# Buffers by name, a mask in the first norm, paired squares and a new order in a two-layer convolution block

## The chip, the cores and the metric

The kernel runs on one core of a Trainium2 chip. The metric is the device time of one execution in microseconds (us), a median over several runs; the profile is of one further execution. The engines are TensorE (PE; PEld is its weight load), VectorE (DVE), ScalarE (ACT), GpSimd (POOL) and SyncE (SP), which here issues the DMAs. All data are float32; a float32 product appears in the trace as two records of PE.

## What is computed

The input x has the shape 4 x 128 x 128 x 128 (batch, channel, row, column). Layer 0 is, cut to what matters:

```python
def _block(t):                       # t: tokens (pixels) x 128 channels
    t = _ln(t)                       # with gain ln0_g and shift ln0_b
    y1 = _ln(t)
    t = t + (sigmoid(y1) * y1) @ W_out.T
    wht = _ln(t) @ W_whiten.T
    k = square(relu(wht @ W_key.T))  # 512 wide
    return t + sigmoid(wht @ W_recep.T) * (k @ W_value.T)

x = x + _L0(_gn(x))                  # _gn: group norm, 32 groups of 4 channels
x = x + _L1(_gn(x))                  # 3x3 convolution times a gate of the means
```

`_L0` adds the block of the image and the block of the turned image, turned back; since the block works on each pixel alone, both are the same. Layer 1 is a 3x3 convolution with a bias, multiplied by a squeeze-and-excite gate.

## The kernel before

An image of the batch has 16384 pixels: 32 chunks of 512 pixels. Two chunks make a group g (64 groups, 16 for each image). `layer0(g)` emits the operations of a group, once for each of its two chunks h: the group norm's scale and shift on a copy of the block that is loaded with its pixels turned (`u`, tile xd), a 32x32 transpose on DVE (`ut`), three layer norms (`bn0` to `bn2` on DVE, then eps on ACT, a power -0.5 on POOL, the shift on POOL), each norm applied by ACT (`t`, `z`), gain and bias (`g`, `b`), a transpose of z on PE (`Tz`) or, from group 22 on, through DRAM, silu on ACT, the attention product (`att`), and then on [channel, pixel] tiles: four key products (`pk`, 128 x 512), relu on ACT (`re`), squares on ACT or DVE (`sq`, `sqd`), the receptance product (`pr`) with its tanh on ACT (`th`, tile r), four value products (`kv`) that accumulate into one bank, the gate on DVE (`q`), and two additions into the resident block of x on POOL (`S`, `x1`). `R` is the reciprocal deviation of the third norm spread over all partitions. For groups 0 and 1 the gain and bias stand on DVE instead of POOL.

Before group 0 the statistics of image 0 are needed. `first_stats` loads it as eight tiles xf of 1 MB and DVE takes their statistics (`in0`); after tiles 6 and 7 it also emits three and two "hot" products on PE, which read the tile, write into a bank called fill and serve no result. `input_norm(b)` turns the statistics of an image into a scale and a shift: `gag` aggregates per channel (DVE), `gpm` averages the means over groups of 4 channels (PE), `gsp` forms mean squares (DVE), `gpv` averages these (PE), then eps, power and shift. Since the turned block needs the values of four channel quarters in four columns, `gpm` and `gpv` multiply by four matrices `gturn[:, q]`, one product for each column; `gpm` has a fifth product by `gmat`. The images 1 to 3 get their norm while the image before is worked on.

`conv_setup(b)` does the like for layer 1 and scales its weights, and `conv(k)` computes the convolution of a block of 16 rows by a transform over rows: DVE forms v0 to v5, PE multiplies (three products of about 512 columns each, tile m), ACT and DVE put the outputs together, SP stores. Convolution blocks of image b run among the groups of image b + 1; those of the last image run alone at the end, where tiles v are put into slots of the pool h and products into the banks of all the pools (TAIL_BANKS).

The order of all this is not written by hand. Each operation is registered with an engine, a cost, a priority (its group number plus an entry of the table SHIFT for its kind), what it reads and writes, and the tiles that it opens. `Plan.order` plays the program with these costs, always takes for the engine that comes free next the operation with the best priority among those that can start soon (LOOK and HASTE weigh lateness), and the instructions are emitted in this order, each engine's in its own queue. The semaphores follow from the data. ROOM gives the number of buffers of each pool. In the order of before, the buffers of a pool are taken in turn: the k-th tile of a pool waits until the tile that was opened ROOM[pool] places earlier is free. While the planned time is below 330 us, `busy` puts fill products (of `gturn` by `gmat`) into the planned gaps of PE, except ahead of `gpm` and the hot products.

SQUARES says for each chunk h and key product j whether the square is done on DVE ("D") or ACT ("A"): in groups 0 to 16 j = 0, 1 on DVE and j = 2, 3 on ACT, later all on ACT, each as an operation of its own on 512 elements in a tile h of which there are six.

Lines that the prediction names: L411 fill, L493 aggregate, L498 and L500 the products of the first norm, L509 to L527 its small steps, L757 the scale on ACT, L820 powers, L839 the layer norms applied, L942 the transpose of z, L954 att, L1033 pk, L1038 relu, L1044 and L1050 the square on ACT and on DVE, L1058 pr, L1063 tanh, L1071 kv, L1080 the gate, L1086 and L1026 additions on POOL, L1182 a v of the convolution, L1203 to L1205 its products. The core of `input_norm` before:

```python
def grouped(key, src, own):
    pm = T[key]
    for q in range(SUB):
        nc.tensor.matmul(pm[:, q : q + 1], gturn[:, q], src, start=True, stop=True)
    if own:
        nc.tensor.matmul(pm[:, SUB : SUB + 1], gmat, src, start=True, stop=True)
```

Of the kernel before, what the change touches and what calls it, by code (L numbers as in the profile page):

```python
# [13 lines left out]
P = 128  # L14
# [9 lines left out]
    "R": -94.694, "Rc": 15.085, "Rm": -2.646, "S": 24.009, "T": -84.8, "Tz": -36.19, "W": -22.14,  # L24
    "ab": 37.315, "att": 1.644, "b": 31.731, "bn0": 11.794, "bn1": -17.35, "bn2": -15.592,
    "bx": 49.609, "c": 7.82, "cag": 6.719, "cav": -18.068, "cd": -103.804, "cp": -37.768,
    "cp1": -27.368, "cpm": -17.233, "cpr": -71.755, "cpv": -65.194, "cre": 48.407, "crt": -73.005,
    "csg": -26.086, "csp": -39.311, "cth": -29.247, "cve": 53.942, "e": 12.136, "e0": 14.7,
    "e1": -70.81, "e2": -55.971, "edge": 60.492, "fw": 14.887, "g": -16.106, "gag": -13.379,
    "gnb": -14.148, "gpm": -2.701, "gpv": -23.531, "grt": -1.635, "gsp": -6.989, "gve": -30.013,  # L30
    "hot": -13.329, "in": 26.361, "in0": 105.375, "kv": 3.816, "late": 12.753, "m0": 23.5,
    "m1": -101.213, "o": -54.585, "pk": 3.497, "pq": -18.954, "pr": 3.288, "q": -106.007,
    "raw": -61.508, "rc": -6.337, "re": -93.796, "silu": -97.676, "sq": -115.033, "sqd": -34.912,
    "t": -2.49, "tD": -49.255, "tR": 16.588, "tW": -20.948, "th": -60.823, "tt": 105.266,
    "u": 16.271, "us": -19.465, "ut": 67.807, "ut2": 9.337, "uw": -50.513, "v": 57.985, "w": 117.982,
    "w0": 44.736, "w1": -43.048, "w2": -6.943, "x": 70.181, "x1": -70.076, "xc": 6.78, "xd": 2.407,
    "xf": -58.371, "xo": -10.863, "xs": -54.606, "y": 24.867, "z": 15.121, "zD": 21.243,
    "zR": 18.813, "zW": -13.966,
}
SQUARES = (("DDAA", "DDAA"), ("AAAA", "AAAA"))  # L40
# [3 lines left out]
LOOK = {'PE': 0.018, 'DVE': 0.087, 'ACT': 0.048, 'POOL': 0.004, 'SP': 0.048}  # L44
HASTE = 31.975
SQUARES_AT = 17
ROOM = dict(
    x=3, xd=2, xs=2, ut=3, t=7, z=2, y=2, zd=2, zc=2, td=2, tt=2, R=2, y2=2, h=6, r=2, xc=2, vt=3, v=4,
# [3 lines left out]
BACKLOG = 1.96  # L52
FIRST_U_ON_DVE = (2, 3)


XF_BUS, FIRST_XD, LATE_AT = 3.4, -25, -5
FILL_UNTIL, FILL_STEP = 330, 1.2
FIRST_FILL = {6: 3, 7: 2}
# [30 lines left out]
class Plan:  # L89
# [34 lines left out]
    def order(self):  # L124
# [14 lines left out]
        freed, queue, taken = {}, {}, {}  # L139
# [12 lines left out]
        def slots(o):  # L152
            at = 0.0
            count = {}
            for t in o["new"]:
                tag = self.home[t]
                k = taken.get(tag, 0) + count.get(tag, 0)
                count[tag] = count.get(tag, 0) + 1
                if k >= self.room[tag]:
                    old = queue[tag][k - self.room[tag]] if k - self.room[tag] < len(queue[tag]) else None  # L160
                    if old is None or pending[old]:
                        return INF
                    at = max(at, freed[old])
            return at

        while done < n:
# [54 lines left out]
            for t in o["new"]:  # L221
                tag = self.home[t]
                queue.setdefault(tag, []).append(t)
                taken[tag] = taken.get(tag, 0) + 1
            for t in touches[i]:
                pending[t] -= 1
                freed[t] = max(freed.get(t, 0.0), en)
            for j in after[i]:
                reach = (self.OWN if ops[j]["eng"] == e else self.REACH)[ops[j]["eng"]]
                ready[j] = max(ready[j], en + reach)  # L230
                left[j] -= 1
                if not left[j]:
                    waiting[ops[j]["eng"]].append(j)
# [9 lines left out]
def conv_preact_kernel(  # L243
# [42 lines left out]
        z=[P, SUB, C], y=[P, CH], y2=[P, CH], h=[P, CH], r=[P, CH],  # L286
# [10 lines left out]
    def make(t, tag):  # L297
        pool = ps if tag[0] == "B" else sb
        T[t] = pool.tile(SHAPE[tag], F32, tag=tag, name=t[0], bufs=ROOM[tag])
        return T[t]  # L300

    def bank(name):
        return ps.tile([P, CH], F32, tag="Bh", name=name, bufs=ROOM["Bh"])

    def staged(name, n, src=None):
        t = sb.tile([P, n], F32, tag="h", name=name, bufs=ROOM["h"])
        if src is not None:
            nc.scalar.dma_start(t, src)
        return t

    vec = sb.tile([5, C], F32, tag="vt", name="vec", bufs=ROOM["vt"])
# [3 lines left out]
    for name, src in (("g0row", ln0_g), ("b0row", ln0_b)):  # L315
        row0.append(sb.tile([1, C], F32, tag="y2", name=name, bufs=ROOM["y2"]))
# [3 lines left out]
    wo = sb.tile([P, P], F32, tag="v", name="wo", bufs=ROOM["v"])  # L320
# [26 lines left out]
    gmat = gmat.rearrange("p a b -> p (a b)")  # L347
    gturn = const.tile([P, SUB, P], F32, tag="gturn", name="gturn")
    for q in range(SUB):
# [3 lines left out]
        )  # L353

# [10 lines left out]
    ones = sb.tile([1, P], F32, tag="r", name="ones", bufs=ROOM["r"])  # L365
    nc.gpsimd.memset(ones, 1.0)

    warm = sb.tile([P, 1], F32, tag="r", name="warm", bufs=ROOM["r"])
# [38 lines left out]
    fill = ps.tile([P, CH], F32, tag="Bconv", name="fill", bufs=ROOM["Bconv"])  # L407
# [14 lines left out]
    READ, WRITE = (0, 0.85), (0, 0.4)  # L422

    def op(name, eng, cost, prio, emit, reads=(), writes=(), new=(), port=False, bus=0.0):
        return plan.op(name, eng, cost, prio + SHIFT.get(name, 0.0), emit, reads, writes, new, port, bus)
# [58 lines left out]
    def input_norm(b, at):  # L484
# [5 lines left out]

        def aggregate():
            S["mv"] = col("mv0", 2)
            nc.vector.bn_aggr(S["mv"], st0.pop(b).rearrange("p n s -> p (n s)"))  # L493

        def grouped(key, src, own):
            pm = T[key]
            for q in range(SUB):
                nc.tensor.matmul(pm[:, q : q + 1], gturn[:, q], src, start=True, stop=True)  # L498
            if own:
                nc.tensor.matmul(pm[:, SUB : SUB + 1], gmat, src, start=True, stop=True)  # L500

        def means():
            make(("pm0", b), "Bh")
            grouped(("pm0", b), S["mv"][:, 0:1], True)

        def spread():
# [5 lines left out]
            S["q"] = q  # L512

        def variances():
            make(("pv0", b), "Bh")
            grouped(("pv0", b), S["q"], False)
# [12 lines left out]

        step("gag", V, (0.4, 0.5), aggregate, [(s, i) for i in range(NCH)], [(("gnv", b), 0)])  # L530
        step("gpm", E, (0.5, 0.55), means, (), [(("pm0", b), 0)], [(("pm0", b), "Bh")])
        step("gsp", V, (0.65, 0.75), spread, [(("pm0", b), 0)])
        step("gpv", E, (0.4, 0.45), variances, (), [(("pv0", b), 0)], [(("pv0", b), "Bh")])
# [4 lines left out]
    def conv_setup(b, at):  # L538
# [7 lines left out]
        def small(name, eng, cost, fn, bank=None):  # L546
            t = (name, b)
            step(name, eng, cost, fn, (), [(t, 0)] if bank else (), [(t, "Bh")] if bank else ())
# [58 lines left out]
        small("csp", V, (0.8, 0.9), spread)  # L607
        small("cpv", E, (0.1, 0.15), variances, True)
        small("cve", V, TINY, with_eps)
# [3 lines left out]
        small("cre", V, (0.2, 0.3), rect)  # L613
        small("cpr", E, (0.3, 0.35), second, True)
        small("cth", A, (0.6, 0.75), tanh)
# [120 lines left out]
    def layer0(g):  # L736
# [3 lines left out]
        if p * PAIR % PER == 0:  # L740
# [6 lines left out]
            for q in range(SUB):  # L747

                on_dve = k == 0 and q in FIRST_U_ON_DVE

                def lay(q=q, on_dve=on_dve):
                    rs, nb = gn0[b]
                    scale, bias = rs[:, q : q + 1], nb[:, q : q + 1]
                    if on_dve:
                        nc.vector.tensor_scalar(T[xd][:, q], T[xd][:, q], scale, bias, ALU.mult, ALU.add)
                    else:
                        nc.scalar.activation(T[xd][:, q], T[xd][:, q], AF.Identity, bias=bias, scale=scale)  # L757

                op(
                    "u", V if on_dve else A, (0.61, 0.7) if on_dve else (0.705, 0.82), g, lay, [(("gn0", b), 0), *((xd, a) for a in range(SUB))],  # L760
                    [(xd, ("u", q))],
                )
# [11 lines left out]
        def norm(n, src):  # L774
            st, rs, nb = ("st", n, g), ("rs", n, g), ("nb", n, g)
            eps = ceps[:, 0:1] if n == 0 else ceps[:, 1:2]
            for h in range(PAIR):
                op(
# [3 lines left out]
            if n == 2 and not R_ON_PE(g):  # L782
# [13 lines left out]
                def store(a):  # L796
                    if a == 0:
                        T[rd] = dram.tile([SUB, N, 32], F32, tag="rd", name="rd", bufs=ROOM["rd"])
# [12 lines left out]
            for hs in parts:  # L811
                part = slice(hs[0] * SUB, (hs[-1] + 1) * SUB)
# [30 lines left out]
        def to_channels(name, src, td, tc_, h):  # L843
# [16 lines left out]
            def store(a):  # L860
                if a == 0:
                    T[ds_] = dram.tile([P, SUB, PAIR, P], F32, tag=name + "s", name=name + "s", bufs=ROOM[name + "s"])
# [17 lines left out]
        for h in range(PAIR):  # L880
            r = (p * PAIR + h) % PER

            def turn(h=h, r=r):
# [5 lines left out]
                "ut", V, (0.61, 0.7), g, turn, [(xd, ("u", q)) for q in range(SUB)],  # L889
# [3 lines left out]
        for h in range(PAIR):  # L893
            t = ("t", g, h)
# [21 lines left out]
        for h in range(PAIR):  # L916
            t, z, zt, y, att = (("t", g, h), ("z", g, h), ("zt", g, h), ("y", g, h), ("att", g, h))
# [8 lines left out]
        for h in range(PAIR):  # L926
            t, z, zt, y, att = (("t", g, h), ("z", g, h), ("zt", g, h), ("y", g, h), ("att", g, h))
# [36 lines left out]
        if R_ON_PE(g):  # L964
            for h in range(PAIR):
                rp = ("rp", g, h)
# [22 lines left out]
        for h in range(PAIR):  # L989
            r = (p * PAIR + h) % PER  # L990
# [4 lines left out]
        for h in range(PAIR):  # L995
# [325 lines left out]
```

## Time and profile before

| | |
|---|---|
| median of 3 runs | 1744.41 us (1743.2 to 1745.63) |
| the profiled execution | 1742.63 us |
| its span, first to last instruction | 1740.9 us |
| granted TensorE clock, mean | 0.997 |
| PE records kv, pk (1024 each), busy | 525.8 and 480.9 us |
| PE records of the convolution (L1203 to L1205), busy | 588.0 us |
| PE records att, pr, busy | 132.8 and 132.3 us |
| ACT relu (512) and square (444), busy | 336.1 and 267.5 us |
| DVE square (68), mean | 740 ns |
| DMA | 354.66 MB, 204 GB/s |

Busy times are unions of records; a record of a product is longer than its step to the next[...]. Idle time of an engine that is not the bound costs nothing. The waits that the views name are put down to the semaphore that came last.

### The profile page before, as it was taken

Reading aid. Unit: us, or ns where it says so; the run is one execution under the profiler, and the core shown is the slowest. Engines: PE = TensorE matmul, PEld = TensorE weight load, DVE = VectorE, ACT = ScalarE, POOL = GpSimd, SP = SyncE. Lnnn points to the kernel's source line nnn. Section 1 sums busy time; section 2 is a strip of 40 time slices with the busy share of each in tenths; the row PEclk is TensorE's granted clock in tenths of the full one; section 3 lists DMA queues with packets and bytes.
Section 4 is the critical chain, followed back from the end, with each engine's and each line's share of the span. In section 5 each row is a group of like instructions: output and inputs, shape, how many; then the busy total and the mean of one; then the engine's idle time right before and its main releaser. Section 6 shows DMA issues by size and latency. Waiting matters only on the chain.

```text
span 1740.9 us, 18709 instructions
## 1 busy us (share of the span) xinstructions
PE 1690.7 (97%) x4872; PEld 815.7 (47%) x4872; DVE 1424.9 (82%) x2619; ACT 1293.8 (74%) x2656; POOL 1184.0 (68%) x1085
## 2 busy tenths in 40 slices
PE   5899999999999999999999999999999999999999
PEld 2444544444444445444445445454544444444443
DVE  5898888788889967798998887888897766448986
ACT  1999998898988887889889877998887875440000
POOL 1778887788987885879777886988878773310000
PEclk9999999999999999999999999999999999999999
DMA  9366675466577777578778877577776565215321
GB/s 326 91 213 202 193 219 194 145 206 230 153 250 246 252 230 236 199 232 247 250 245 245 254 238 240 178 218 236 241 254 199 183 204 176 101 75 224 154 98 73
DMA packets 140170, 354.66 MB, mean 204 GB/s; under 512 B 19079, under 2 KB 78750, under 8 KB 122782
## 3 DMA queue, kind: packets, MB, share of 16 engines
q1 hardware_dynamic: 139472, 352.99, 63.1%
q8 instruction: 39, 0.64, 0.2%
q14 instruction: 69, 0.57, 0.1%
q10 hardware_dynamic: 590, 0.46, 0.1%
HBM read 230.31 MB, written 123.07 MB: 203 GB/s over the span
## 4 chain that ended last, share of the span: by engine, by line
PE 71%; ACT 10%; POOL 8%; DVE 7%; DMA 2%; issue 2%; SPq 0%; ACTq 0%; DVEq 0%; POOLq 0%
PE kv L1071 19%; PE pk L1033 18%; PE m L1203 7%; PE m L1204 7%; PE m L1205 7%; PE att L954 5%; PE pr L1058 5%; ACT t L839 2%; ACT h L1038 2%; POOL rs L820 2%; ACT z L839 2%; DVE st L770 1%; ACT h L1044 1%; POOL x L1026 1%; POOL t L908 1%
## 5 line engine op out<-in xcount | busy, mean ns | idle before, releaser
L1071 PE MATMUL kv<-h,wv 128*128 128x512 f32 x1024 | 525.8, 598 | 4.6 <-DVE r L1080 2.6
L1033 PE MATMUL pk<-y,wk_s 128*128 128x512 f32 x1024 | 480.9, 595 | 4.7 <-ACT h L1038 3.1
L1038 ACT ACTIVATE h<-pk,kbias 128x512 f32<-128x512 f32 x512 | 336.1, 682 | 90.9 <-PE pk L1033 88.3
L1033 PEld LDWEIGHTS pk<-y,wk_s 128*128 128x128 f32 x1024 | 190.0, 190 | 239.3 <-issue 178.1
L1071 PEld LDWEIGHTS kv<-h,wv 128*128 128x128 f32 x1024 | 183.0, 190 | 205.3 <-issue 164.1
L1044 ACT ACTIVATE h<-h 128x512 f32<-128x512 f32 x444 | 267.5, 629 | 2.6
L1086 POOL TENSOR_TENSOR x<-x,r 128x512 f32<-128x512 f32 x128 | 169.8, 1327 | 132.0 <-DVE r L1080 128.5
L820 POOL TENSOR_TENSOR rs<-rs,nhalf 128x8 f32<-128x8 f32 (+1 forms) x134 | 227.2, 1700 | 47.3 <-ACT rs L817 45.1
L839 ACT ACTIVATE z<-t,nb,rs 128x128 f32<-128x128 f32 x512 | 208.7, 489 | 21.8 <-POOL nb L825 20.9
L839 ACT ACTIVATE t<-ut,nb,rs 128x128 f32<-128x128 f32 x512 | 209.7, 488 | 8.5 <-POOL nb L825 4.8
L908 POOL TENSOR_TENSOR t<-t,g 128x512 f32<-128x512 f32 x124 | 161.2, 1301 | 68.0 <-ACT t L839 67.6
L770 DVE BATCH_NORM_STATS2 st<-t 128x6 f32<-128x256 f32 x512 | 187.1, 410 | 22.9 <-POOL t L911 22.7
L1203 PE MATMUL m<-v,uw 128*128 128x512 f32 x384 | 197.7, 596 | 3.9 <-DVE v L1182 3.9
L1204 PE MATMUL m<-v,uw 128*128 128x508 f32 x384 | 195.4, 590 | 0.0
L1205 PE MATMUL m<-v,uw 128*128 128x508 f32 x384 | 194.9, 589 | 0.0
L1015 POOL TENSOR_TENSOR y<-tt,R 128x512 f32<-128x512 f32 x96 | 130.9, 1367 | 59.8 <-PE pk L1033 46.9
L1026 POOL TENSOR_TENSOR x<-tt,x 128x512 f32<-128x512 f32 x124 | 162.5, 1324 | 3.9 <-DMA tt<-ts 3.7
L911 POOL TENSOR_TENSOR t<-t,b 128x512 f32<-128x512 f32 x124 | 162.7, 1319 | 2.6
L954 PEld LDWEIGHTS att<-wo,y 128*128 128x128 f32 x1024 | 130.9, 192 | 51.7 <-issue 33.1
L1063 ACT ACTIVATE r<-pr,rbias 128x512 f32<-128x512 f32 x128 | 87.1, 681 | 72.6 <-PE pr L1058 36.2
L1058 PE MATMUL pr<-y,wr_s 128*128 128x512 f32 x256 | 132.3, 600 | 3.9 <-ACT h L1038 3.0
L954 PE MATMUL att<-wo,y 128*128 128x128 f32 x1024 | 132.8, 276 | 0.4 <-ACT y L947 0.3
(160 smaller groups left out, 2278.6 us busy)
## 6 DMA issues: line engine op xcount, KB each, us to landing
xd<-in_x SPq DMA_DIRECT2D x128, 256.0 KB
x<-in_x SPq DMA_DIRECT2D x32, 1024.0 KB
xo<-x SPq DMA_DIRECT2D x32, 1024.0 KB
R<-rd SPq DMA_DIRECT2D x63, 512.0 KB
ts<-td SPq DMA_DIRECT2D x248, 128.0 KB
tt<-ts SPq DMA_DIRECT2D x62, 512.0 KB
out<-xc SPq DMA_DIRECT2D x31, 1024.0 KB
xc<-xo SPq DMA_DIRECT2D x24, 1152.0 KB
```

Source lines behind the costliest of these rows:

```text
L770: nc.vector.bn_stats(st[:, i : i + 2, :].rearrange("p n f -> p (n f)"), two)
L820: nc.gpsimd.tensor_tensor(T[rs][:, part], T[rs][:, part], nhalf[:, :k], ALU.pow)
L839: nc.scalar.activation(dst[:, s, :], src[:, s, :], AF.Identity, bias=nb[:, i : i + 1], scale=rs[:, i : i + 1])
L954: nc.tensor.matmul(pa[:, ts(m, P)], T[y][:, ts(m, P)], wo2, start=True, stop=True)
L1033: nc.tensor.matmul(make(pk, "Bh"), wk_s[:, ts(j, P)], T[y2], start=True, stop=True)
L1038: nc.scalar.activation(make(hh, "h"), T[pk], AF.Relu, bias=kbias[:, j : j + 1])
L1044: nc.scalar.activation(T[hh], T[hh], AF.Square)
L1058: nc.tensor.matmul(make(pr, "Bh"), wr_s, T[y2], start=True, stop=True)
L1071: nc.tensor.matmul(T[kv], wv[:, j, :], T["h", g, h, j], start=(j == 0), stop=(j == NH - 1))
L1203: nc.tensor.matmul(pc, u[:, 1], vv, start=True, stop=False)
L1204: nc.tensor.matmul(pc[:, :, 1:W], u[:, 0], vv[:, :, 0 : W - 1], start=False, stop=False)
L1205: nc.tensor.matmul(pc[:, :, 0 : W - 1], u[:, 2], vv[:, :, 1:W], start=False, stop=True)
```

## The change

It consists of these parts.

- Each tile of a pool is bound to a slot that `Plan.order` chose: the plan keeps a list of free slots of each pool with the time at which each came free, takes the earliest one, and the tile is then allocated under the slot's own name with one buffer. The setup's tiles take slots in turn (`early`); the staged weights go into the pool t instead of h.
- The first norm multiplies the channel means by a mask `own` (128 x 4, one column for each quarter of 32 channels) and uses one product by `gany`, the sum of the four `gturn` matrices, where it had four products. The planner's costs of these steps change too.
- The hot products are gone (`FIRST_FILL` is empty).
- Tiles h hold two key products side by side (three tiles of 1024 in place of six of 512). SQUARES gets a form "W": one ACT instruction squares both halves. Groups 0 to 16: "DAWW" for chunk 0, "DDWW" for chunk 1; later groups "WWWW".
- LAG lowers the priority number of the chunks of groups 0 and 1, chunk by chunk, so that they go first.
- The tiles v of the last image's convolution lie in slots of t.
- The steps of `conv_setup` name their bank among what they read. The scale `u` is registered by row piece; with the values set it is emitted as before (two quarters on ACT, two on DVE for the first block).
- All of SHIFT, and LOOK, HASTE, BACKLOG and XF_BUS, have new values, so the order of every queue is new.

```diff
-SQUARES = (("DDAA", "DDAA"), ("AAAA", "AAAA"))
+SQUARES = (("DAWW", "DDWW"), ("WWWW", "WWWW"))
...
-LOOK = {'PE': 0.018, 'DVE': 0.087, 'ACT': 0.048, 'POOL': 0.004, 'SP': 0.048}
-HASTE = 31.975
+LOOK = {'PE': 0, 'DVE': 0.072, 'ACT': 0.176, 'POOL': 0, 'SP': 0.106}
+HASTE = 51.55
...
-FIRST_FILL = {6: 3, 7: 2}
+FIRST_FILL = {}
+LAG = {(0, 0): -400, (0, 1): -200, (1, 0): -60, (1, 1): -30}
+FIRST_U = (((0, 4), "AADD"),)
...
+        spare = {tag: [(0.0, i) for i in range(n)] for tag, n in self.room.items()}
...
-                k = taken.get(tag, 0) + count.get(tag, 0)
-                count[tag] = count.get(tag, 0) + 1
-                if k >= self.room[tag]:
-                    old = queue[tag][k - self.room[tag]] if k - self.room[tag] < len(queue[tag]) else None
-                    if old is None or pending[old]:
-                        return INF
-                    at = max(at, freed[old])
+                k = count.get(tag, 0)
+                count[tag] = k + 1
+                if k >= len(spare[tag]):
+                    return INF
+                at = max(at, spare[tag][k][0])
...
+                self.slot[t] = spare[self.home[t]].pop(0)[1]
...
+                if not pending[t]:
+                    spare[self.home[t]].append((freed[t], self.slot[t]))
+                    spare[self.home[t]].sort()
...
-        T[t] = pool.tile(SHAPE[tag], F32, tag=tag, name=t[0], bufs=ROOM[tag])
+        T[t] = pool.tile(SHAPE[tag], F32, tag=f"{tag}-{plan.slot[t]}", name=t[0], bufs=1)
...
+    gany = const.tile([P, P], F32, tag="gany", name="gany")
+    nc.gpsimd.tensor_tensor(gany, gturn[:, 0], gturn[:, 1], ALU.add)
+    for q in range(2, SUB):
+        nc.gpsimd.tensor_tensor(gany, gany, gturn[:, q], ALU.add)
...
+        def split(name, src):
+            S[name] = col(name, SUB)
+            nc.vector.tensor_scalar(S[name], own, src, None, ALU.mult)
+
         def aggregate():
             S["mv"] = col("mv0", 2)
             nc.vector.bn_aggr(S["mv"], st0.pop(b).rearrange("p n s -> p (n s)"))
...
+            split("m4", S["mv"][:, 0:1])
...
-            make(("pm0", b), "Bh")
-            grouped(("pm0", b), S["mv"][:, 0:1], True)
+            pm = make(("pm0", b), "Bh")
+            nc.tensor.matmul(pm[:, :SUB], gany, S["m4"], start=True, stop=True)
+            nc.tensor.matmul(pm[:, SUB : SUB + 1], gmat, S["mv"][:, 0:1], start=True, stop=True)
...
-            make(("pv0", b), "Bh")
-            grouped(("pv0", b), S["q"], False)
+            nc.tensor.matmul(make(("pv0", b), "Bh")[:, :SUB], gany, S["q4"], start=True, stop=True)
...
-                pk, hh = ("pk", g, h, j), ("h", g, h, j)
+                pk, hh = ("pk", g, h, j), ("h", g, h, j // 2)
...
+                elif how == "W" and not first:
 
                     def square(hh=hh):
-                        nc.scalar.activation(T[hh], T[hh], AF.Square)
...
+                        x = T[hh].rearrange("p a b -> p (a b)")
+                        nc.scalar.activation(x, x, AF.Square)
+
+                    op("sq", A, WIDE, g, square, [(hh, 0), (hh, 1)], [(hh, 0), (hh, 1)])
...
-                t = sb.tile([P, CH], F32, tag="h", name=n, bufs=ROOM["h"])
+                t = sb.tile([P, CH], F32, tag=f"t-{plan.slot[name_of(n)]}", name=n, bufs=1)
```

## The prediction

> **What bounds the kernel now.** I read the page first (shares of the engines, then the chain that ended last), then the busy time of each engine in stretches of 50 us, then the chain and the timelines of the first 80 us, then the waits of TensorE. The page:
>
> ```profile
> PE 1690.7 (97%) x4872; PEld 815.7 (47%) x4872; DVE 1424.9 (82%) x2619; ACT 1293.8 (74%) x2656; POOL 1184.0 (68%) x1085
> ...
> PE 71%; ACT 10%; POOL 8%; DVE 7%; DMA 2%; issue 2%; SPq 0%; ACTq 0%; DVEq 0%; POOLq 0%
> ```
>
> TensorE is busy 97% of the span and holds 71% of the chain. Only two things can shorten this kernel: less work on TensorE, or fewer holes in it. The stretches show where the holes are (columns: stretch, its length, then busy us and instruction counts of PE, PEld, DVE, ACT, POOL; granted clock; DMA):
>
> ```profile
> 0.00:50.00 50.00, 28.78 (x77) 15.57 (x78) 28.20 (x52) 13.39 (x35) 7.39 (x27) 1.00 0.86 288
> 50.00:100.00 50.00, 43.06 (x175) 24.00 (x174) 45.54 (x98) 49.22 (x114) 41.91 (x51) 0.97 0.47 132
> 100.00:150.00 50.00, 47.51 (x152) 23.51 (x151) 44.17 (x84) 47.24 (x99) 40.50 (x39) 1.00 0.71 210
> ...
> 300.00:350.00 50.00, 46.76 (x145) 23.09 (x144) 39.23 (x76) 41.83 (x88) 37.04 (x35) 0.97 0.44 137
> ...
> 1100.00:1150.00 50.00, 50.00 (x141) 23.69 (x141) 43.97 (x86) 46.04 (x100) 46.07 (x41) 1.00 0.58 182
> ...
> 1600.00:1650.00 50.00, 46.58 (x106) 20.45 (x106) 44.74 (x77) 3.82 (x6) 0.00 (x0) 0.97 0.37 144
> ```
>
> From 500 to 1600 us TensorE has no hole to speak of (2.8 us in sum). The holes are in the start. Of the PE time in the first two stretches 17.8 and 6.4 us are fill products (the same view for the tile `fill` alone), which compute nothing. Between 50 and 350 us idle and fill together make about 23 us, another 3.5 us lie between 350 and 500, and 3.4 at 1600. Before 50 us TensorE does no chunk work at all. What ends last there is seen in the chain of the first stretch (start, us, what):
>
> ```profile
> 29.63 7.06 PE fill L411 x10
> 36.69 0.79 PE pm L498 x8
> 37.48 0.24 PE pm L500 x2
> 37.74 0.18 DVE mg L509
> ...
> 38.50 1.04 PE pv L498 x8
> 39.56 0.17 DVE rs L520
> 39.80 1.03 POOL rs L523
> 40.83 4.11 issue
> ```
>
> and in the timelines of DVE and of PE:
>
> ```profile
> 31.04 1.02 DVE L493 BATCH_NORM_AGGREGATE mv<-st 128x2 f32<-128x192 f32 x1
> ...
> 29.21 0.42 PE L404 MATMUL pb<-b,raw 128*128 128x1 f32 x2
> 29.49 7.20 PE L411 MATMUL fill<-xf,gmat 128*128 128x512 f32 x10
> 39.38 13.12 PE L411 MATMUL fill<-gturn,gmat 128*128 128x512 f32 x30
> 54.00 1.50 PE L942 MATMUL zt<-ident,z 128*128 128x128 f32 x4 [1.50 <-ACT z L839]
> ```
>
> The aggregated mean is ready at 31.04 + 1.02 = 32.06. The product that averages it over its group starts at 36.53, because five "hot" fill products (ten records) stand before it in TensorE's queue. They hold the chain 4.5 us. Everything later (the scale of the first block, 41.06) hangs on it.
>
> **The change part by part.**
>
> *Hot fill removed* (`FIRST_FILL` empty). The first product no longer queues behind 7.2 us of fill. I follow the new chain from 32.06: the mask multiply 0.16 (row L520, a TENSOR_SCALAR of 128x4, takes 0.16) with its step, 32.25; two products, four records on an array that has idled, at the price of the pair at 29.21 (0.42 for two), 0.85, with a handover 33.15; the three DVE steps that lay between 37.74 and 38.35 (0.61) and the second mask multiply 0.19, 33.95; handover 0.15 and one product 0.42, 34.55; then rs, power and nb as between 39.56 and 41.02 (1.46), so that the first block's scale starts at about 36.1 in place of 41.06: **-5.0 us**, of which 4.5 is the fill and 0.5 the fewer products. The block itself is no obstacle: in the trace the 2 KB packets of the first turned block are in by about 30.4 us, and SP's x loads, which waited 2.1 us for the hot fill to release its tile, come earlier. POOL's new mask and summed matrix (three adds of 128x128 at 0.45, row L364, and small ones, under 2 us) fall into POOL's idle 35.6 us before 39.80, hidden.
>
> A rule of the Trainium skill speaks against this: "TensorE: Matmul & The Clock Gate", Part 1, says that the array is throttled to half rate until it has been busy for some 3.4 us, so fill products buy speed. The row agrees that warming exists: ten records in 7.20 us here, thirty in 13.12 later, 0.72 against 0.44 each, so 2.8 us were lost to a cold array. By the rule alone the second fill now pays these 2.8 us. By the row the first transpose of z found TensorE idle for 1.50 us (54.00), so 2.8 - 1.5 = 1.3 us could show, if as many fill products are issued. Between 0 and 2.8 I take **+1.0**, near the row.
>
> *One product for four.* Each group norm had 4 + 1 + 4 products and has 1 + 1 + 1. Six products of two records go; their records follow each other at 0.11 us (eight in 1.02), so 1.33 us per norm. The first is in the chain above; the other three lie where TensorE is full: **-4.0 us**. The eight new DVE mask multiplies (0.16 each) stand in a DVE that is 82% busy and add 0.3 us to a norm that is asked for groups ahead; zero, and at most 0.3 x 3 if that cover is gone.
>
> *Squares in pairs.* A square of 512 costs ACT 0.52 us back to back (two in 1.04 in the chain). No row has 1024 elements. Two singles, 1.04, are the upper end; the copies of 512 and 128 elements (L398: 0.577 and 0.258) give 0.83 ns an element, so 0.52 + 0.425 = 0.945 is what I take. In groups 0 to 16 the squares go from four on DVE and four on ACT (2.08 us) to three on DVE, one single and two pairs on ACT (2.41): ACT +0.33 a group, DVE -0.6 (the step of L1050). A group of these takes TensorE about 18 us, in which ACT idles 0.7 to 1.0 us between 100 and 250 us (47.2 to 48.1 of 50). It fits, narrowly. From group 17 on ACT saves 8 x 0.52 - 4 x 0.945 = 0.38 a group, 18 us in all, which is worth nothing where TensorE is at 50.00 of 50. A pair does delay its first kv product by one relu (0.58) and half a square: queued behind it on ACT are the next relus, and on PE the kv. Other products stand between; zero, between 0 and 17 x 0.9 = 15 us if nothing covers it.
>
> *Named buffers, the new order, the lag of groups 0 and 1.* The buffers add no instruction. A tile may take whichever slot came free first instead of the oldest one's. Which waits of before come from the rotation no view says; waits that look like it (ACT r on POOL x, 33.2 us in 23) are on ACT, not on TensorE, whose own waits after 54 us make some 22 us in all. The lag puts the first chunk ahead of all others. In the trace its first key product stands at 71.08, 30 us after the scale. Its own steps, added by their rows (scale, transpose, stats, power, shift, normalise, gain and bias, again to z, transpose, silu, attention, norm, R) make about 20 us, so key work can start 8 to 10 us sooner relative to the scale. TensorE's idle and fill in 50 to 100 us is 13.4 us, and the chain between 71 and 86 us runs through DVE back to back, which loses a square per group. Not all is won: with ACT at 49.2 of 50 what chunk 0 gains others give. Between -14 (all of that hole, and a little after it) and +10 (a worse order elsewhere: every queue, SP's and POOL's too, is newly sorted) I take **-5.0**, a fifth of the 23 us.
>
> *The tail.* The last batch's v tiles go from six h slots to seven t slots. The 3.4 us hole at 1608 waits for DVE v, not for a slot. Zero, from -3.4 to +3.
>
> **Sum.** -5.0 + 1.0 - 4.0 - 5.0 = -13.0. The profiled execution took 1742.63 us (span 1740.9 and 1.7 around it), 1.8 below the median of the runs, 1744.41. So 1729.6 in its terms and 1731.4 by the median: I say **1731**.
>
> **The rivals.**
> *Only the sure parts count* (chance 0.18): the order gives nothing, because slots come free in turn anyway and ACT's 49.2 of 50 in the ramp decides. For it: ACT gains work exactly there. Against it: the idle of TensorE in 50 to 100 us is behind a DVE chain. Time: 1744.4 - 8 = 1736.
> *The ramp closes* (0.14): the early chunk and the order take most of the 23 us, and TensorE is full from 65 us on. Time: 1744.4 - 8 - 13 = 1723.
> *ACT and the paired squares starve TensorE in the first 17 groups* (0.12). Place: kv L1071 and pk L1033 waiting for ACT h between 60 and 350 us. Price: 0.33 us of ACT and 0.9 us of latency a group, 17 x 1.2 = 20 us, less the sure 8: 1756 at full price, 1750 at about two thirds. It decides from the point at which ACT has no idle left, about 0.9 us more per group than now. Against it: 0.33 is a third of that.
> My forecast has 0.56.
>
> **Chances.** A measurement of this kernel can tell about 0.2%, 3.5 us, from no change: 1740.9 to 1747.9. Faster: 0.55 of the forecast, 0.14 of the ramp, 0.13 of the sure parts: 0.82. Same: 0.01 + 0.05 + 0.02 = 0.08. Slower: 0.10. Range 1720 to 1743: below lies little of the ramp case, above the slow case; without that case 1723 to 1738.
>
> **What would show it.** Right: the first pm product within 1 us of the end of the aggregation, the first xd scale at 36 to 37 us, 8 pm, 8 pv and 8 gmat records in place of 32, 32 and 8, a first key product before 62 us, PE at 50 of 50 from 100 us on, ACT's pair square near 1.03 us long and 0.95 apart. Wrong: the scale still near 41 us (a load that was hidden); the second fill ending after the first z is ready (the cold array costs more than 1 us); waits of kv or pk for ACT h of more than 10 us between 60 and 350 us (the third rival); new holes in 500 to 1600 us, where I count on none; or PE's busy time falling by less than the fill and 5 us.

## The result and the profile after

The changed kernel takes 1791.43 us (median of 4 runs, 1790.96 to 1794.17) against 1743.81 before: ratio 1.0279, 95% interval 1.026 to 1.0298. It is slower by 47 us where I forecast 12 us less. The profiled execution took 1794.17 us. Its page:

```profile
span 1792.4 us, 18617 instructions
PE 1721.4 (96%) x4860; PEld 818.2 (46%) x4860; DVE 1405.6 (78%) x2610; ACT 1288.4 (72%) x2451; POOL 1177.0 (66%) x1091
...
PE 64%; POOL 14%; DVE 8%; ACT 7%; DMA 4%; issue 3%; SPq 0%; ACTq 0%; DVEq 0%; POOLq 0%
```

TensorE is busy 31 us more (1690.7 before) with less to do, and its share of the chain fell from 71 to 64%: the chain now runs more through POOL (8 to 14%). The stretches that answer to those of before:

```profile
0.00:50.00 50.00, 25.47 (x60) 13.35 (x60) 33.26 (x64) 17.68 (x45) 12.59 (x40) 1.00 0.97 306
50.00:100.00 50.00, 40.34 (x144) 21.36 (x145) 36.99 (x80) 42.02 (x94) 37.36 (x44) 0.97 0.38 97
100.00:150.00 50.00, 44.81 (x178) 26.62 (x177) 36.06 (x79) 38.84 (x83) 30.01 (x31) 0.92 0.55 163
...
900.00:950.00 50.00, 47.04 (x129) 22.47 (x130) 36.20 (x62) 35.64 (x64) 27.70 (x26) 0.97 0.76 235
...
1600.00:1650.00 50.00, 45.78 (x110) 20.29 (x110) 35.68 (x68) 6.69 (x12) 3.46 (x3) 0.97 0.52 205
```

and one long stretch, first after, then before:

```profile
350.00:1600.00 1250.00, 1233.47 (x3452) 580.85 (x3450) 988.42 (x1823) 990.89 (x1846) 932.84 (x825) 1.00 0.68 210
350.00:1600.00 1250.00, 1243.67 (x3536) 596.67 (x3535) 1021.08 (x1868) 993.10 (x2019) 931.40 (x815) 1.00 0.67 216
```

From 100 to 150 us every engine has idle time at once (ACT 38.8, DVE 36.1, POOL 30.0 of 50): nothing is short of capacity, the work is in an order in which each waits for another. Idle and fill together in 50 to 350 us are now 44 us (23 before), idle in 350 to 1600 us 16.5 (6.3 before), in 1600 to 1700 6.7 (3.4 before). That is 35 us. The rest does not show as idle: PE's records follow each other more slowly. Summed over all records, what the distance from start to start exceeds the usual step of their width (0.43 us for 512 columns, 0.11 for 128) is 119 us against 77 before; without the idle, which is in both, it is 58.2 against 37.5, so 21 us more. By an estimate from the same records a third of these 21 us lies where the granted clock was 0.5; most of the rest is slack too short to show as idle, since a record is longer than its step. The prediction counted work and holes and, apart from one slow fill, had no term for this.

The start itself went nearly as forecast. The timeline of PE after:

```profile
32.51 0.56 PE L527 MATMUL pm<-m,gany 128*128 128x4 f32 x2 [0.95 <-DVE m L518]
...
34.98 14.39 PE L434 MATMUL fill<-gturn,gmat 128*128 128x512 f32 x28
49.59 1.48 PE L975 MATMUL zt<-ident,z 128*128 128x128 f32 x4 [0.23 <-ACT z L868]
53.14 1.16 PE L987 MATMUL att<-wo,y 128*128 128x128 f32 x8 [1.21 <-ACT y L980]
...
62.60 1.88 PE L1069 MATMUL pk<-y,wk_s 128*128 128x512 f32 x4
...
82.87 9.61 PE L434 MATMUL fill<-gturn,gmat 128*128 128x512 f32 x22
96.82 5.40 PE L1069 MATMUL pk<-y,wk_s 128*128 128x512 f32 x8 [4.35 <-DVE y L1051]
```

and before:

```profile
36.53 0.95 PE L498 MATMUL pm<-mv,gturn 128*128 128x1 f32 x8
...
57.55 1.72 PE L954 MATMUL att<-wo,y 128*128 128x128 f32 x8 [0.34 <-ACT y L947]
...
71.08 1.88 PE L1033 MATMUL pk<-y,wk_s 128*128 128x512 f32 x4
```

The first norm's product starts at 32.51 (36.53 before), the first key product at 62.60 (71.08). Then, at 83 us, group 0 is through, and for 14 us TensorE has nothing of use: 9.6 us of fill and 4.35 of idle. Before, it was busy with products for 12.8 of the same 14 us. The chain of that hole:

```profile
85.23 1.61 POOL four L819
86.84 1.76 POOL t L942 x2
...
90.88 1.64 POOL rs L849
...
92.99 1.66 ACT t L868 x4
...
94.67 0.72 DVE ut L916
...
95.42 0.76 DVE st L797 x2
96.18 0.60 DVE y L1051
...
96.82 3.35 PE pk L1069 x4
```

TensorE waits for the key input y of group 1. In DVE's queue y stands behind a transpose `ut` and its statistics; `ut` waits 3.7 us for ACT's t, and ACT's t waits for powers and shifts in POOL's queue. This is the wait that ends last, but a second one ends shortly before it. y also needs R, which PE spreads for group 0 alone; from group 1 on it is written to DRAM and read back. The statistics for it end at 83.58, its power on POOL (`four`) at 86.84, and then

```profile
91.12 0.34 SPq L1020 DMA_DIRECT2D R<-rd  x1
```

The packets of this load end at 94.6 in the trace. A free DVE queue would thus have brought y forward by about 1.5 us at most (an estimate: 96.18 less 94.6); most of the hole is the way of R, in which the order, with group 0 through, had no other product ready. A second hole, again before y, follows at 147 us.

### The profile page after: what moved, and what is told of

It reads as the page before. It is cut to its first block, busy times and chain, and to the rows that moved or that the text cites. A ratio compares the mean times of both kernels' runs of the same rounds, so it can differ in the third digit from the quotient of the medians.

```text
span 1792.4 us, 18617 instructions
## 1 busy us (share of the span) xinstructions
PE 1721.4 (96%) x4860; PEld 818.2 (46%) x4860; DVE 1405.6 (78%) x2610; ACT 1288.4 (72%) x2451; POOL 1177.0 (66%) x1091
## 4 chain that ended last, share of the span: by engine, by line
PE 64%; POOL 14%; DVE 8%; ACT 7%; DMA 4%; issue 3%; SPq 0%; ACTq 0%; DVEq 0%; POOLq 0%
PE pk L1069 17%; PE kv L1127 16%; PE m L1260 7%; PE m L1261 7%; PE m L1262 7%; PE att L987 5%; PE pr L1114 4%; POOL rs L849 3%; ACT t L868 2%; POOL t L942 2%; ACT z L868 2%; POOL t L939 2%; POOL four L819 2%; ACT h L1075 1%; POOL y L1051 1%
## 5 line engine op out<-in xcount | busy, mean ns | idle before, releaser
L1069 PE MATMUL pk<-y,wk_s 128*128 128x512 f32 x1024 | 509.3, 599 | 11.7 <-DVE y L1051 7.6
L1075 ACT ACTIVATE h<-pk,kbias 128x512 f32<-128x512 f32 x512 | 340.4, 679 | 99.7 <-PE kv L1127 55.0
L1094 ACT ACTIVATE h<-h 128x1024 f32<-128x1024 f32 x222 | 233.7, 1053 | 2.0
L1051 POOL TENSOR_TENSOR y<-tt,R 128x512 f32<-128x512 f32 x96 | 126.7, 1326 | 92.6 <-PE pr L1114 52.4
L1136 DVE SCALAR_TENSOR_TENSOR r<-r,kv 128x512 f32<-128x512 f32 x128 | 86.5, 675 | 82.7 <-PE kv L1127 80.1
```

Of the source, the lines that this page charges most:

```text
L1069: nc.tensor.matmul(make(pk, "Bh"), wk_s[:, ts(j, P)], T[y2], start=True, stop=True)
L1075: nc.scalar.activation(dst[:, j % 2], T[pk], AF.Relu, bias=kbias[:, j : j + 1])
L1094: nc.scalar.activation(x, x, AF.Square)
```

## The experiments

I started with three theories: the lag of groups 0 and 1 (1), the new priorities (2), the paired squares (3). Where no other number is given, times are medians and the ratio is to the kernel before on the same chip.

**The lag out.**

```diff
-LAG = {(0, 0): -400, (0, 1): -200, (1, 0): -60, (1, 1): -30}
+LAG = {}
```

> The changed kernel with the lag of groups 0 and 1 taken out, all else as changed. Theory 1 (the lag lets groups 0 and 1 run so far ahead that groups 2 to 5 start late and TensorE runs dry at 82 and at 118 us): the holes before 200 us go, about 30 us come back, 1755 to 1765 us. Theory 2 (the new priorities of the kinds of operation are at fault): little changes, above 1780. Theory 3 (the paired squares are at fault): little changes, above 1780.

1794.61 us, ratio 1.0283 (1.0266 to 1.0299). Theory 1 falls as I put it. The holes at 83 and 118 us do go, but another comes at the change of image:

```profile
439.85 1.63 PE L975 MATMUL zt<-ident,z 128*128 128x128 f32 x4 [5.55 <-ACT z L868]
```

**The old priorities, lag out** (the tables are named here, not printed).

```diff
-LAG = {(0, 0): -400, (0, 1): -200, (1, 0): -60, (1, 1): -30}
+LAG = {}
-SHIFT, LOOK, HASTE, BACKLOG, XF_BUS of the changed kernel
+SHIFT, LOOK, HASTE, BACKLOG, XF_BUS of the kernel before
```

> The changed kernel with the lag taken out and with the priorities, look-ahead, haste, backlog and bus time of the kernel before; named buffers, mask norm, no hot fill and paired squares stay. Theory 1 (lag): as without the lag alone, 1755 to 1765. Theory 2 (new priorities): all of the loss comes back and the start's gain shows, 1730 to 1740. Theory 3 (paired squares): stays above 1770.

1783.36 us, 1.0217 (1.0197 to 1.0238). Only a fifth of the loss comes back. The old numbers do little better with the new parts: theory 2 falls as I put it.

**The old squares.**

```diff
-SQUARES = (("DAWW", "DDWW"), ("WWWW", "WWWW"))
+SQUARES = (("DDAA", "DDAA"), ("AAAA", "AAAA"))
```

> The changed kernel with the squares of the kernel before (two single ones on DVE and two on ACT for each chunk of groups 0 to 16, four single ones on ACT later), in the tiles of two; all else as changed, with the lag. Theory 3 (a pair must wait for its second relu and holds its tile longer, so kv waits): 1750 or less. Theories 1 and 2: within 10 us of the changed kernel, 1780 to 1800.

1798.23 us, 1.0304 (1.0286 to 1.0322). Theory 3 falls as I put it. Each of these three runs also got a new order from the planner, so none of them prices its part alone.

**The kernel before with the two parts I held sure** (no hot fill; mask, summed matrix and their planner's costs).

```diff
-FIRST_FILL = {6: 3, 7: 2}
+FIRST_FILL = {}
...
+            split("m4", S["mv"][:, 0:1])
...
-        step("gag", V, (0.4, 0.5), aggregate, [(s, i) for i in range(NCH)], [(("gnv", b), 0)])
+        step("gag", V, (1.2, 1.3), aggregate, [(s, i) for i in range(NCH)], [(("gnv", b), 0)])
...
```

> The kernel before with two parts of the change alone: no hot fill, and the mask with one product in the first norm. Order, buffers and squares as before. By the terms of the prediction's sum that I held sure (-5.0 at the start, +1.0 for the cold array, -4.0 for the products) 1736, whichever theory holds for the rest; if a cheaper start is given back in the ramp, 1740 to 1744.

1763.34 us, 1.0115 (1.0093 to 1.0138): 19 us slower, with a start as in the prediction (the norm's products at 33.5 us). No theory of mine had this. Of the two parts, one takes out operations on which nothing hangs, and the other changes four costs and removes work. What is left is the plan: its greedy choice runs through 7700 operations, and a first different choice changes all later ones. So theory 4: the parts are cheap, and what costs time is the new order that any edit makes the planner deal, for which the table of priorities is not fitted. Theory 5, its rival: the earlier start or the cold array does harm by itself. Four runs tell them apart.

**The planner's four costs alone**: every instruction as before, the order not (on PE it differs from the 280th of 1548 operations on).

```diff
-        step("gag", V, (0.4, 0.5), aggregate, [(s, i) for i in range(NCH)], [(("gnv", b), 0)])
-        step("gpm", E, (0.5, 0.55), means, (), [(("pm0", b), 0)], [(("pm0", b), "Bh")])
+        step("gag", V, (1.2, 1.3), aggregate, [(s, i) for i in range(NCH)], [(("gnv", b), 0)])
+        step("gpm", E, (0.4, 0.45), means, (), [(("pm0", b), 0)], [(("pm0", b), "Bh")])
...
```

> The kernel before with four numbers of the planner alone: its costs of the aggregation, the two products and the spread of the first norm are those of the changed kernel. Every instruction is the same as before, in number and shape; only the order in the queues differs. Theory 4: slower by what b_sure lost and a little more, since nothing is saved: 1764 to 1775. Theory 5: no change, 1742 to 1748.

1768.91 us, 1.0144 (1.013 to 1.0158). Theory 4 holds: 25 us are lost without any change of what is computed. Between 350 and 1600 us TensorE idles 25.0 us in this run, 6.3 in the kernel before. Two stretches hold 10.8 us of it:

```profile
500.00:550.00 50.00, 45.30 (x140) 22.32 (x140) 40.36 (x78) 31.65 (x65) 32.60 (x29) 1.00 0.67 206
800.00:850.00 50.00, 43.89 (x112) 19.40 (x112) 47.45 (x84) 33.27 (x68) 36.39 (x32) 0.97 0.70 221
```

and those of the kernel before:

```profile
500.00:550.00 50.00, 50.00 (x142) 24.16 (x141) 46.27 (x88) 41.61 (x91) 44.43 (x41) 1.00 0.76 236
800.00:850.00 50.00, 50.00 (x146) 24.39 (x146) 43.92 (x90) 43.45 (x90) 43.48 (x39) 1.00 0.79 247
```

In the second stretch DVE is nearly full, and its chain shows with what:

```profile
831.86 1.06 DVE uw L621 x2
832.91 0.60 DVE q L1180
833.51 0.67 DVE st L770 x2
...
838.62 2.95 DVE uw L627 x4
```

DVE scales the convolution's weights (uw) and begins a convolution block, while the statistics of the next chunks stand behind; ACT and POOL fall to 33 and 36 of 50, and TensorE waits 3.6 us for y. The work is the same in both kernels; here it meets at a bad moment.

**No hot fill alone**: no operation of the plan hangs on these products, so every queue keeps its order.

```diff
-FIRST_FILL = {6: 3, 7: 2}
+FIRST_FILL = {}
```

> The kernel before without the hot fill products and nothing else; the order of every queue stays as it is, since no operation of the plan hangs on them. Theory 4 (the parts themselves are as cheap as the prediction's sum says, and what costs time is that any edit of the list of operations makes the planner deal a new order, for which the priorities do not fit): about -4, 1738 to 1742. Its rival, theory 5 (the earlier start or the cold array makes the ramp itself worse): 1750 or more, as in the two sure parts run together.

1740.72 us (21 runs), 0.9986 (0.9978 to 0.9994). Theory 5 falls for this part.

**The same two parts as in b_sure with the order of before**: the hot operation stays in the plan and emits nothing, the mask norm is planned with the old costs.

```diff
-                    busy(times, T[t][:, : CH // W, :].rearrange("p r w -> p (r w)"))
+                    pass
...
+            split("m4", S["mv"][:, 0:1])
+            pm = make(("pm0", b), "Bh")
+            nc.tensor.matmul(pm[:, :SUB], gany, S["m4"], start=True, stop=True)
...
```

> The kernel before without the hot fill and with the mask and one product in the first norm, but planned with the costs of before, so that every queue keeps the order of before. Theory 4: the sum of the sure parts, 1734 to 1739. Theory 5: as b_sure, about 1763.

1738.84 us (11 runs), 0.9972 (0.9963 to 0.998). The same instructions in the dealt order of b_sure took 1763.34. Theory 4 holds, and the sure parts are worth 5 us (3.5 to 6.5).

**The changed kernel's numbers on the kernel before** (named likewise).

```diff
-SHIFT, LOOK, HASTE, BACKLOG, XF_BUS of the kernel before
+SHIFT, LOOK, HASTE, BACKLOG, XF_BUS of the changed kernel
```

> The kernel before with the priorities, look-ahead, haste, backlog and bus time of the changed kernel; hot fill, rotating buffers, four products and single squares as before, no lag. Theory 4: the new numbers were not fitted to this list of operations either, 1755 to 1790. Theory 2 (the new numbers themselves are bad): 1780 or more.

1773.27 us, 1.0172 (1.0158 to 1.0186). The new table does not fit the old list either.

**Named buffers alone**, all numbers of before.

```diff
-        T[t] = pool.tile(SHAPE[tag], F32, tag=tag, name=t[0], bufs=ROOM[tag])
+        T[t] = pool.tile(SHAPE[tag], F32, tag=f"{tag}-{plan.slot[t]}", name=t[0], bufs=1)
...
-                if k >= self.room[tag]:
-                    old = queue[tag][k - self.room[tag]] if k - self.room[tag] < len(queue[tag]) else None
...
+                if k >= len(spare[tag]):
+                    return INF
+                at = max(at, spare[tag][k][0])
```

> The kernel before with named buffers alone: slots chosen by the planner, all numbers of before, hot fill, four products and single squares. The instructions are those of before. Theory 4: a tile may open earlier than in turn, so the planner deals another order, and the old table does not fit it: 1765 to 1795. The prediction's view (a freer choice of slots can only help): 1735 to 1744.

1790.49 us, 1.0282 (1.0263 to 1.03): this one part alone loses as much as the whole change. The first place where its order departs is an att that may open its bank earlier, in group 0; on PE 1387 of 1548 operations then stand elsewhere. Its deepest hole, around 850 us, shows where the new order leads; the chain:

```profile
846.33 0.43 SPq L872
846.81 5.37 DMA tt<-ts
852.34 1.28 POOL y L1023
853.65 2.07 PE pr L1066 x2
```

SP issues the read of the turned tile at 846.3 us, the transfer takes 5.4 us, POOL's y waits for it, and TensorE for y (5.2 us), after which its first records follow each other 0.85 us apart in place of 0.43. The stretch in this run, then in the kernel before (granted clock 0.93 and 1.00):

```profile
850.00:900.00 50.00, 46.34 (x136) 23.19 (x137) 39.17 (x79) 41.90 (x81) 40.17 (x36) 0.93 0.71 231
850.00:900.00 50.00, 50.00 (x141) 23.88 (x140) 45.31 (x83) 44.29 (x95) 39.59 (x35) 1.00 0.76 242
```

**Named buffers, mask and no hot fill with the order of before**: the slots are chosen after the order is fixed.

```diff
         self.result, self.end = result, end
+        self.slot, spare = {}, {tag: [(0.0, k) for k in range(m)] for tag, m in self.room.items()}
...
+        for _, i in result:
+            for t in ops[i]["new"]:
+                self.slot[t] = spare[self.home[t]].pop(0)[1]
```

> As b_pinned (order of before in every queue, no hot fill, mask norm), and the tiles named: the slots are chosen after the order is fixed, each time the one that came free first by the plan. It differs from b_pinned by names alone. Theory 4 (a named buffer costs nothing, the order it lets the planner deal does): as b_pinned, 1736 to 1742. If names cost time as such (other waits at a reused slot): 1750 or more.

1737.29 us (13 runs), 0.9956 (0.994 to 0.9972), the interval overlapping that of b_pinned. Names cost nothing that shows; with the order that they let the planner deal they cost 47 us. These two runs, which can't be told apart, are the fastest of the study, ahead of both kernels.

**The changed kernel with a table fitted to it**, lag out.

```diff
-LAG = {(0, 0): -400, (0, 1): -200, (1, 0): -60, (1, 1): -30}
+LAG = {}
-SHIFT = {"R": -140.667, "Rc": -0.44, ...
+SHIFT = {"R": -220.862, "Rc": 13.852, ...
...
```

> The changed kernel (named buffers, mask norm, no hot fill, paired squares; without the lag of groups 0 and 1) with a new table of priorities, look-ahead, haste and backlog, found by some 5600 random edits that were kept when the planner's own account of the program got shorter; no instruction differs in kind from the run without the lag. Theory 4 (no part is dear, the loss is in priorities that do not fit the list of operations): the loss of 47 us goes, 1730 to 1745. Theory 3 and its like (named buffers or paired squares cost time in themselves): 1755 or more.

1749.77 us, 1.004 (1.0027 to 1.0054). Of the loss without the lag, 50 us, some 44 are gone by numbers of the table alone. It misses my range by 5 us and stays behind the kernel before. Idle of TensorE in 350 to 1600 us is 9.2 us where the run without the lag had 25.0.

**b_sure with a fitted table** (named likewise).

```diff
-SHIFT, LOOK, HASTE, BACKLOG of the kernel before
+SHIFT, LOOK, HASTE, BACKLOG found by trial
...
```

> The kernel before without the hot fill and with the mask norm, planned with the changed costs as in b_sure, and a table found in the same way by some 4600 edits. Theory 4: the 19 us that b_sure lost are won back and the parts' gain shows, 1733 to 1743. If a_fit ends lower than this, named buffers and pairs are worth the difference.

1746.07 us (21 runs), 1.0013 (1.0003 to 1.0022). Some 16 of the 19 us come back; the time is above my range by 3. A table that the planner likes is not the chip's best: both fitted orders lie 7 to 11 us behind the order of before with the same or similar parts (b_pinned). The 0.27% between a_fit and b_fit I can't give to the buffers or the pairs: each has another table.

**What the plan itself said.** I overlooked that every kernel file holds a forecast of its order: the time at which `Plan.order`, playing the program with its costs, ends the last operation. It needs no chip (us):

| kernel | end of the plan | measured |
|---|---|---|
| before; b_no_hot, b_pinned and b_pinned_named, which keep its order | 1707.5 | 1744; 1741, 1739, 1737 |
| b_sure; b_costs (the same costs) | 1721.4 | 1763; 1769 |
| b_new_order | 1721.0 | 1773 |
| a_old_order | 1733.9 | 1783 |
| changed kernel | 1739.6 | 1791 |
| b_named | 1741.6 | 1790 |
| a_squares | 1743.8 | 1798 |
| a_no_lag | 1747.8 | 1795 |
| b_fit | 1706.6 | 1746 |
| a_fit | 1701.7 | 1750 |

The plan already has the changed kernel 32 us longer than the kernel before. All eight orders dealt under a table not fitted to their list are longer in the plan too, by 13.5 to 40.3 us; the chip added 5 to 17 to that. For the two fitted tables it promised 1 and 6 us less and the chip gave 3 and 6 more, so it tells a bad order, and not which of two good ones is better.

## Why the prediction was wrong

*The step that failed* is the term for named buffers and the new order, put at -5.0 us between -14 and +10. Its argument, that the buffers add no instruction and that a tile may take the slot that is free first, is right and beside the point: with the order held the names cost nothing that shows (b_pinned_named), with the order dealt anew they alone make +2.8% (b_named): +47 us, as much as the whole change, where the term had -5.0. The order of before is one deal that its table fits, with 2.8 us of idle between 500 and 1600 us. In every run whose planner chose freely under a table not fitted to its list the loss is 1.2 to 3.0%: four costs, another table, names, squares, lag in or out. I had priced a worse order at +10 us at most from nothing that the trace shows; a trace of one order says nothing of the spread of orders. What I needed was the end of the new plan, which said +32, or a run of the old instructions in another order, such as b_costs, which gave +25. What remains open is what the pairs cost in themselves, within a loss that the table alone brings from 50 to 6 us.

*The rival that ended slower* named another mechanism, ACT and pairs starving TensorE in the first 17 groups. The changed kernel does not show it: all of PE's waits for ACT h in the whole run are these two, 3.7 us in sum (the same two made 6.1 before),

```profile
PE pk L1069 <- ACT h L1075: 2.8, 5, 1.1
PE pr L1114 <- ACT h L1075: 0.9, 1, 0.9
```

and single squares, in yet another order, did not help.

*The start.* -5.0 forecast for the scale of the first block; on DVE it starts at 36.69 in place of 41.08, -4.4. The timeline of DVE after:

```profile
30.99 1.02 DVE L522 BATCH_NORM_AGGREGATE mv<-st 128x2 f32<-128x192 f32 x1
32.13 0.23 DVE L518 TENSOR_SCALAR m<-own,mv 128x4 f32<-128x4 f32 x1
33.53 0.17 DVE L533 COPY mg<-pm 128x5 f32<-128x5 f32 x1 [1.17 <-PE pm L528]
...
36.69 1.00 DVE L780 TENSOR_SCALAR xd<-xd,rs,nb 128x512 f32<-128x512 f32 x2
```

From the end of the aggregation (32.01) to the scale it took 4.7 us, and the added-up chain had 4.0. Most of the difference lies ahead of the first copy: the mask multiply took 0.23 and not 0.16 and started 0.12 late, and from its end to the copy, with the two products between, 1.17 us passed in place of 0.90.

*The cold array* (+1.0, from 0 to 2.8): the second fill did run slowly, 28 records in 14.39 us, 0.51 each against 0.44, about 2 us. It hid: z was ready within 0.23 us of its end, and the first attention product came 4.4 us earlier (53.14, before 57.55), as much as the scale. The term was nearer 0.

*One product for four* (-4.0). pm and pv records are busy 1.6 us each in the changed kernel, 3.9 and 4.0 before; three quarters of the 4.7 is 3.5. In measured time b_pinned and b_no_hot differ by 0.14%, 2.4 us, with overlapping intervals. Start and products together were -8 in the sum; b_pinned measured 5.0. These terms were right in kind and, at 5.0 (3.5 to 6.5) of 8, mis-sized; what became of the rest is not settled, since b_pinned's idle between 350 and 1600 us is 10.7 us in its profile (6.3 before).

*Squares in pairs.* Cost right: 1053 ns long in the mean, 0.95 apart in the chain, for a forecast of 1.03 and 0.945. That latency is hidden was taken at zero; no run isolates it, as none had pairs in the order of before. It stays open.

*The lag.* The first key product came at 62.60, 25.9 us after the scale where it was 30.0 before: sooner by 4.1 us, and not by the 8 to 10 that the added-up 20 us of steps would give; "before 62 us" was missed. I had written that what chunk 0 gains others give, and then credited a gain. The stretch from 80 to 160 us gave back more than it won: TensorE has 37 us of idle and fill there, 4.5 before. Yet taking the lag away did not help either, since the table then dealt a hole elsewhere.

*The tail*, zero between -3.4 and +3: +3.3 us of idle in 1600 to 1700 us. Two waits make 6.0 of the 6.7 us after:

```profile
1644.00 2.05 PE L1260 MATMUL m<-v,uw 128*128 128x512 f32 x2 [3.53 <-DVE v L1239]
...
1663.58 1.68 PE L1260 MATMUL m<-v,uw 128*128 128x512 f32 x2 [2.51 <-DVE v L1239]
```

Both are for DVE's v, as was the one wait before (3.42), and no view names a slot. The stretches don't hold quite the same work either, since the changed kernel is some 50 us behind by then.

## What to carry to other kernels

Where a planner deals the order by priorities, an edit has two prices: its own and that of the deal it sets off; here they were -5 us and about +25 to +47. Read the end of the new plan before anything else. Then measure the first price with the order held (keep the plan's list and costs, change what is emitted) and the second with the instructions held (change a cost alone), and forecast no order from a trace of another. In a kernel whose TensorE is busy 97% of the span, a freer planner won nothing here, even with tables fitted to the plan's own account; whether a table fitted on the chip would, no run shows.

## What the runs showed of the hardware that I had not expected

A hole costs more than its length. After holes of 1.5 to 5.2 us TensorE's granted clock fell: to 0.92 in the changed kernel's stretch from 100 to 150 us and to 0.93 in that of b_named from 850 to 900 (1.00 before in both). In the changed kernel one such fall follows an idle of 1.46 us at 135 us and eight transposes that ACT feeds one by one. The attention products then come at half pace, 16 records in 3.78 us, where the next 16 take 2.05:

```profile
140.00 3.78 PE L987 MATMUL att<-wo,y 128*128 128x128 f32 x16 [0.19 <-ACT y L980]
...
145.51 2.05 PE L987 MATMUL att<-wo,y 128*128 128x128 f32 x16
```

The granted clock from 140 to 143.5 us was 0.50. Over the whole span the mean clock went from 0.997 to 0.993, by an estimate from these two the worth of some 7 us of the 47.
